# A graph network's first layer: node sums added one supertile later, edge products one group ahead, and a count check moved to ScalarE

## The chip, the core and the metric

The kernel runs on one core of one Trainium2 chip. The core has five engines with queues of their own, which work in order and wait for each other on semaphores: TensorE (PE; its weight loads are shown as PEld), VectorE (DVE), ScalarE (ACT), GpSimd (POOL) and SyncE (SP, here only a queue for transfers). The metric is the device time of one execution in microseconds; less is better. A profile is one further execution, recorded instruction by instruction.

## What is computed

Four graph layers over 6250 nodes with 64 features and 206250 edges sorted by destination (each node has itself as an edge too). Each layer's result is added to x and normalised. The change is in layer 0:

```python
def _L0_gnn_ref(H, Xe, id_Xe, M_W, M_b, U_W, U_b):
    features = H[id_Xe[0]]
    M_in = jnp.concatenate([features, Xe], axis=1)
    Y = jax.nn.relu(M_in @ M_W.T + M_b)
    Z = jax.ops.segment_sum(Y, id_Xe[1], num_segments=H.shape[0])
    U_in = jnp.concatenate([H, Z], axis=1)
    return jax.nn.relu(U_in @ U_W.T + U_b)

x = _layernorm(x + _L0_gnn_ref(x, edge_attr_64, edge_index, ...), axis=-1)
x = _layernorm(x + _L1_gnn_ref(x, edge_index, ...), axis=-1)   # two graph convolutions
x = _layernorm(x + _L2_gnn_ref(x, edge_attr_64, src, dst, ...), axis=-1)   # attention over edges
x = _layernorm(x + _L3_gnn_ref(x, edge_index, ...), axis=-1)   # two convolutions, batch norms
```

## The kernel before

**Tiling.** The edges are cut into S = 54 supertiles of L x J = 128 x 30 edges (the last has 91 partitions). Since edges are sorted by destination, a supertile's destinations fit a window of W = 128 nodes. Instructions keep the order in which the program writes them (a manual schedule), so each engine's queue is in program order; pools with 2 or 3 buffers decide how far one engine can run ahead of another.

**Layer 0's loop** (the loop over s at the end of the first printed part) does this for every supertile:

- `fetch_xe` loads 128 x 30 edge rows (one transfer, SP's queue, two buffers), and `fetch_g` gathers 128 x 30 rows of a node table by source: 30 indirect transfers, issued one by one by GpSimd (L433), into one of three buffers g.
- `messages` works on the supertile fetched one iteration earlier, in five groups of six edges a partition. For each group TensorE transposes the edge rows (L662), ScalarE copies the result out of PSUM (L666), TensorE multiplies by the edge weights into pm (L676), and VectorE adds pm's 64 columns to g (L680) and copies four attention columns to we (L682). The transposes run one group ahead of the products. After the five groups ScalarE applies relu to g (L687), and SP stores we to memory for layer 2 (L689).
- `add_window` sums by destination: VectorE makes two one-hot tiles oh, 15 edges a partition each (`one_hot`, L474), TensorE multiplies them with g in 60 instructions into one PSUM tile pa, of which there is one buffer (L484), and VectorE adds pa to the accumulator acc at the window's place (L487).
- In each group, `fill` also runs one step of another job, so that layer 0 and the preparation of later layers share the engines. For the first 11 iterations the job is `degrees`, five supertiles an iteration: two VectorE one-hots oA and oB a step (L524, L527; two buffers each) and 30 small matmuls of the step before (L518). After that it is `adjacency`: 200 steps that build dense count matrices of (source, destination) in one byte a count. A step makes the one-hots (L591, L594; the same oA and oB buffers), multiplies those of the step before (L603, 16 matmuls), has ScalarE cast the products to one-byte floats (L605, four casts), and checks the counts of the step before that.
- `check` (L610) takes on VectorE the largest of the 1568 bytes a partition, read as integers, into a column of most_a; at the end of the kernel this is compared with EXACT, the byte of the largest count that the format holds exactly, 15. Every eighth check is followed by a store of a finished adjacency chunk, on ScalarE's queue (L613). If any check of the kernel fails, a general but slow path at the end computes everything anew; otherwise its loop runs zero times.
- `last_messages` does the last supertile with one-hots made first, and with relu and sums after each group (L684, L700), and then adds pa (L705).

**What comes behind.** Layer 1 and layer 3 are dense products with the count matrices on TensorE (L862). Layer 2 gathers once more for each edge, with GpSimd issuing 30 transfers a supertile.

Of the kernel before, what the change touches and what calls it, by code (L numbers as in the profile page):

```python
# [27 lines left out]
F32 = mybir.dt.float32  # L28
BF16 = mybir.dt.bfloat16
FP8 = mybir.dt.float8e4  # L30
I32 = mybir.dt.int32
I8 = mybir.dt.int8
# [8 lines left out]
LF = 125  # L41
W = 128
R = 64
EXACT = 0x57 + 0.5
BIG = 1.0e30
LN_EPS = 1e-5
BN_EPS = 1e-5
# [8 lines left out]
def tile_gnn_resnorm(ctx: ExitStack, tc, a, out, J):  # L56
# [281 lines left out]
        return min(S, -(-(a_block * (b + 1) + SLACK + R) // LJ)) - 1  # L338

    nc.vector.memset(bad4, 0.0)  # L340

    w_bd = const.tile([128, 2, CW], F32, name="w_bd")
    nc.vector.memset(w_bd, 0.0)
# [82 lines left out]
    def of(s):  # L426

        return LP if isinstance(s, int) and s == S - 1 else L
# [46 lines left out]
                                rel[:, j0:j0 + JH, None].to_broadcast([n, JH, W]), op=OP.is_equal)  # L475
        return oh

    def add_window(ohp, vals, c, rel, base, places=iota):
        n = rel.shape[0]
        pa = sums_in[-1].tile([c, W], F32, name="pa")  # L480
        for j0 in range(0, J, JH):
            oh = one_hot(ohp, rel, j0, places)
            for j in range(JH):
                nc.tensor.matmul(pa, vals[0:n, j0 + j, 0:c], oh[0:n, j, :], start=(j0 + j == 0),  # L484
                                 stop=(j0 + j == J - 1))
        span = acc[0:c, ds(base, W)]
        nc.vector.tensor_add(span, span, pa)  # L487

    def first_of(s):
        why = "a destination, and the accumulator is a window longer than the nodes"  # L490
# [75 lines left out]
    def adjacency(adp, ohd):  # L566
# [40 lines left out]

        def check(c, q0, adj):

            nc.vector.tensor_reduce(most_a[:, (c * L + q0) // QS:(c * L + q0) // QS + 1],  # L610
                                    adj[:, :, :, q0:q0 + QS].bitcast(I8), AX.XYZ, OP.max)
            if q0 + QS == L:
                nc.scalar.dma_start(adj_d[c].bitcast(I8), adj.rearrange("p l a q -> p (l a q)").bitcast(I8))  # L613

# [25 lines left out]
    with st0:  # L640
# [7 lines left out]
            gather(g, D, tab_d, at(src_1 if s < S1 else src_sb, s))  # L648
            return g

        def fetch(s):
            return fetch_xe(s), fetch_g(s)

        def messages(pool, s, xe, g, first_time, fill=lambda: None, then=None):

            m = of(s)
            we = pool.tile([L, J, H], F32, name="we")

            def turned(k):
                pt = ps_t.tile([128, 3, L], F32, name="pt")  # L660
                for i in range(3):
                    nc.tensor.transpose(  # L662
                        pt[:, i, 0:m], xe[0:m, 6 * k + 2 * i:6 * k + 2 * i + 2, :].rearrange("p a c -> p (a c)"),
                        ident[:m, :m])
                xT = pool.tile([128, 3, L], F32, name="xT", bufs=3)
                nc.scalar.copy(xT[:, :, 0:m], pt[:, :, 0:m])  # L666
                return xT[:, :, 0:m]

            xTs = [turned(0)]
            for k in range(J // 6):  # L670
                if k + 1 < J // 6:
                    xTs.append(turned(k + 1))
                xT = xTs.pop(0)
                pm = ps_m.tile([L, 3, 2 * CW], F32, name="pm")
                for i in range(3):
                    nc.tensor.matmul(pm[0:m, i, :], xT[:, i, :], w_bd_f, start=True, stop=True)  # L676
                fill()
                pv = pm[0:m].rearrange("p i (a c) -> p (i a) c", a=2)
                js = slice(6 * k, 6 * k + 6)
                nc.vector.tensor_add(g[0:m, js, :], g[0:m, js, :], pv[:, :, 0:D])  # L680
                if first_time:
                    nc.vector.tensor_copy(we[0:m, js, :], pv[:, :, D:CW])  # L682
                if then:
                    nc.scalar.activation(g[0:m, js, :], g[0:m, js, :], AF.Relu)  # L684
                    then(js)
            if not then:
                nc.scalar.activation(g[0:m], g[0:m], AF.Relu)  # L687
            if first_time:
                nc.sync.dma_start(edges_of(we_d, s), we[0:m])  # L689
            return g  # L690

        def last_messages(s, xe, g):

            rel, n = at(dst_w, s), of(s)
            ohs = [one_hot(ohp, rel, j0, iota_c[:, 0:W]) for j0 in range(0, J, JH)]
            pa = sums_in[-1].tile([D, W], F32, name="pa")

            def add(js):
                for j in range(js.start, js.stop):
                    nc.tensor.matmul(pa, g[0:n, j, :], ohs[j // JH][0:n, j % JH, :], start=(j == 0), stop=(j == J - 1))  # L700

            base = first_of(s)
            messages(l0, s, xe, g, True, then=add)
            span = acc[0:D, ds(base, W)]
            nc.vector.tensor_add(span, span, pa)  # L705

        xes = [fetch_xe(i) for i in range(2)]
        got = xes[0], fetch_g(0)
        load_edges(src_i, src, S1)
        nc.sync.dma_start(hl_d[0:E, :].rearrange("(p i) k -> p i k", p=LF), hl)  # L710
        nc.sync.dma_start(rows_d[E:E + R, :], zero)
# [35 lines left out]

        x_part()

        add0 = lambda v, rel, base: add_window(ohp, v, D, rel, base, iota_c[:, 0:W])  # L750
        with ExitStack() as st1:
            adp = st1.enter_context(tc.tile_pool(name="adp", bufs=2))
            counting = degrees(ohd, list(range(S)))
            building = adjacency(adp, ohd)

            n_count = S // 5 + 1
            n_build = NC * L // QS + 2
            last, done = None, 0
            for s in range(S + 1):
                nxt = got if s == 0 else (xes[1], fetch_g(1)) if s == 1 else fetch(s) if s < S else None  # L760
                if s < n_count:
                    steps = [counting] * 5
                else:
                    upto = -(-n_build * (s - n_count + 1) // (S - n_count))
                    steps, done = [building] * (upto - done), upto

                def fill():
                    if steps:
                        next(steps.pop(), None)

                if s == S:
                    while steps:
                        fill()
                    for _ in building:
                        pass
                    last_messages(s - 1, *last)
                elif last:
                    v = messages(l0, s - 1, *last, True, fill)
                    add0(v, at(dst_w, s - 1), first_of(s - 1))
                while steps:  # L780
                    fill()
                last = nxt
    ps_0.close()
    ps_s = ctx.enter_context(tc.tile_pool(name="ps_s", bufs=2, space=PSUM))
    sums_in.append(ps_s)
# [467 lines left out]


    nc.vector.tensor_reduce(bad4[:, 2:3], most_a, AX.X, OP.max)
    for i, most_ok in enumerate((0.5, R + 0.5, EXACT, 0.5, 0.5)):
        nc.vector.tensor_scalar(bad4[:, i:i + 1], bad4[:, i:i + 1], most_ok, None, op0=OP.is_gt)
    bad1 = small.tile([L, 1], F32, name="bad1")
    nc.vector.tensor_reduce(bad1, bad4, AX.X, OP.max)
# [8 lines left out]
    with tc.For_i(0, n_bad, 1), tc.tile_pool(name="gen", bufs=2) as ag:  # L1268
# [9 lines left out]
        def message_sums(s):  # L1278
            xe = ag.tile([L, J, D], F32, name="xe", bufs=1)
            nc.sync.dma_start(xe[0:of(s)], edges_of(xe_in, s))  # L1280
            g = ag.tile([L, J, D], F32, name="g", bufs=1)
            gather(g, D, tab_d, row_of_edges(ag, src, s))
            windows(s, messages(ag, s, xe, g, False), lambda v, rel, base: add_window(ag, v, D, rel, base))

        all_supertiles(message_sums)

# [53 lines left out]
```

## Time and profile before

| | us |
|---|---|
| median of 3 runs (lowest, highest) | 7077.11 (7062.18, 7077.8) |
| the profiled execution | 5427.65 |
| its span | 5425.9 |
| layer 0's loop within the span | about 101 to 2351 |
| layer 2's gathers within the span | about 2702 to 4830 |

| engine | busy us in the span | share |
|---|---|---|
| GpSimd | 3168.7 | 58% |
| VectorE | 2808.8 | 52% |
| TensorE | 2154.0 | 40% |
| ScalarE | 782.1 | 14% |

In a line of a group or of the timeline stand: the kernel's line, the engine, the operation, what is written and read, partitions x elements, and how many. A group then gives its busy time, the mean of one in ns, and the engine's idle time just before with what ended it. A line of the waits is who waited, for whom, the sum in us, how often, and the longest. "issue" means that the profile shows nothing that the engine waited for; where a wait is long, that includes waits for a buffer that the queue itself carries. GpSimd's busy time is the issuing of a transfer, not the transfer.

### The profile page before, as it was taken

What the parts mean: (1) busy time and instruction counts of PE and PEld (TensorE: products, weight loads), DVE (VectorE), ACT (ScalarE), POOL (GpSimd) and SP (SyncE); (2) the same over time, 40 slices, a digit from 0 to 9 for tenths busy, and PEclk for the clock granted to TensorE, in tenths of its full rate; (3) what the DMA queues carried; (4) which work ended last, traced back from release to release, by engine and by line L of the source; (5) the groups of instructions that cost most, each with busy time, mean ns of one, the idle gap of its engine ahead of it and who ended that gap; (6) DMA issues with size and microseconds to landing.
All of it is one profiled execution on the core that took longest, in us unless ns stands there. A gap on an engine that the chain in (4) does not pass through costs nothing.

```text
span 5425.9 us, 42770 instructions
## 1 busy us (share of the span) xinstructions
PE 2154.0 (40%) x15765; PEld 1667.7 (31%) x15766; DVE 2808.8 (52%) x2743; ACT 782.1 (14%) x1615; POOL 3168.7 (58%) x3350
## 2 busy tenths in 40 slices
PE   2555555555555555589800000000000000019997
PEld 2545554454455445566500000000000000014554
DVE  5888788888878888841213334234243334421102
ACT  0001232232223223221100000000000000001101
POOL 6566767777767776500077777777777777740000
PEclk6766676677677677689955555555555555559998
DMA  4111222222222222247423233233333333335442
GB/s 101 43 47 47 69 72 73 80 72 73 74 78 73 73 68 71 70 173 275 169 68 123 85 112 112 85 123 101 108 101 110 98 102 123 101 101 214 155 167 72
DMA packets 200887, 551.26 MB, mean 102 GB/s; under 512 B 110150, under 2 KB 112466, under 8 KB 178396
## 3 DMA queue, kind: packets, MB, share of 16 engines
q0 software_dynamic: 112336, 219.94, 15.4%
q1 hardware_dynamic: 67908, 281.60, 13.9%
q10 hardware_dynamic: 20424, 46.89, 2.3%
q8 instruction: 126, 2.06, 0.1%
q14 instruction: 93, 0.76, 0.0%
HBM read 442.89 MB, written 105.30 MB: 101 GB/s over the span
## 4 chain that ended last, share of the span: by engine, by line
POOL 36%; PE 19%; issue 18%; DMA 14%; DVE 11%; ACT 2%; DVEq 0%; POOLq 0%; ACTq 0%; SPq 0%
POOL g L433 35%; PE pA L862 12%; DMA rows<-rows_d,first 9%; DMA g<-tab_d,src_sb 5%; PE pa L484 3%; DVE most_a L610 2%; DVE oB L594 2%; DVE oA L591 2%; ACT g L687 1%; DVE g L680 1%; DVE oA L524 1%; PE pm L845 1%; PE pm L189 1%; DVE oB L527 1%; POOL slots L439 0%
## 5 line engine op out<-in xcount | busy, mean ns | idle before, releaser
L433 POOL DMA_INDIRECT g<-tab_d,src_sb x3120 | 2947.9, 945 | 1553.4 <-issue 1044.1
L177 PE MATMUL pt<-ident,acc 128*128 128x128 f32 (+1 forms) x50 | 13.5, 364 | 1994.6 <-DVE acc L235 1994.6
L484 PE MATMUL pa<-oh,g 128*64 128x128 f32 x3180 | 472.6, 324 | 386.0 <-ACT g L687 377.1
L177 PEld LDWEIGHTS pt<-ident,acc 128*128 128x128 f32 (+1 forms) x50 | 7.1, 174 | 1999.8 <-issue 1986.4
L484 PEld LDWEIGHTS pa<-oh,g 128*64 128x64 f32 x3180 | 461.4, 170 | 395.9 <-ACT g L687 395.9
L862 PE MATMUL pA<-adj,three 128*128 128x512 fp8e4 (+3 forms) x2499 | 534.7, 368 | 1.8 <-ACT three L243 1.8
L1010 DVE TENSOR_TENSOR g<-g,we 128x120 f32<-128x120 f32 (+1 forms) x54 | 15.5, 286 | 887.6 <-DMA g<-tab_d,src_sb 887.6
L591 DVE TENSOR_TENSOR oA<-pc,hlT 128x2048 bf16<-128x2048 f32 x200 | 454.7, 2274 | 0.0
L605 ACT CAST adj<-pA 128x392 fp8e4<-128x392 f32 x800 | 350.2, 488 | 590.8 <-PE pA L603 585.8
L603 PE MATMUL pA<-oB,oA 128*128 128x98 bf16 x3200 | 292.1, 241 | 258.2 <-DVE oB L594 189.1
L594 DVE TENSOR_TENSOR oB<-pc,hlT 128x1568 bf16<-128x1568 f32 x200 | 354.5, 1773 | 0.0
L610 DVE TENSOR_REDUCE most_a<-adj 128x1 f32<-128x1568 int8 x200 | 353.7, 1769 | 0.0
L862 PEld LDWEIGHTS <-three 128*96 128x96 bf16 (+1 forms) x2548 | 267.9, 111 | 241.6 <-issue 13.1
L676 PE MATMUL pm<-w_bd,xT 128*128 128x136 f32 (+1 forms) x1620 | 324.7, 351 | 31.0 <-ACT xT L666 14.9
L1040 DVE TENSOR_REDUCE hb<-rows 128x64 f32<-128x4096 f32 x46 | 336.5, 7316 | 0.0
L603 PEld LDWEIGHTS <-oA 128*128 128x128 bf16 x3200 | 227.5, 117 | 322.2 <-DVE oB L594 207.5
L676 PEld LDWEIGHTS pm<-w_bd,xT 128*128 128x128 f32 (+1 forms) x1620 | 276.3, 245 | 61.4 <-DVE we L682 32.9
L1028 ACT COPY same<-pA 128x256 f32<-128x256 f32 x49 | 18.2, 372 | 1813.2 <-DVE pA L1026 1813.2
L1037 DVE TENSOR_TENSOR rows<-rows,pA 128x4096 f32<-128x4096 f32 x49 | 216.7, 4422 | 38.5 <-ACT pA L1035 38.5
L1026 DVE TENSOR_TENSOR pA<-rows,pa 128x256 f32<-128x256 f32 x49 | 21.0, 429 | 414.9 <-DMA rows<-rows_d,first 414.9
L474 DVE TENSOR_TENSOR oh<-pc,dst_w 128x1920 f32<-128x1920 f32 (+1 forms) x108 | 227.1, 2140 | 0.1
L666 ACT COPY xT<-pt 128x384 f32<-128x384 f32 (+1 forms) x270 | 124.0, 479 | 696.9 <-PE pt L662 696.2
(253 smaller groups left out, 2605.0 us busy)
## 6 DMA issues: line engine op xcount, KB each, us to landing
adj<-adj_d SPq DMA_DIRECT2D x100, 1568.0 KB
rows_d<-g SPq DMA_DIRECT2D x53, 1020.0 KB
xe<-in_edge_attr_dram SPq DMA_DIRECT2D x53, 960.0 KB
g<-tab_d,src_sb POOLq DMA_INDIRECT x3120
adj_d<-adj ACTq DMA_DIRECT2D x25, 1568.0 KB
we_d<-we SPq DMA_DIRECT2D x53, 60.0 KB
we<-we_d ACTq DMA_DIRECT2D x53, 60.0 KB
g<-tab_d,src POOLq DMA_INDIRECT x120
```

The lines of the kernel that those rows point to most:

```text
L433: nc.gpsimd.indirect_dma_start(out=g[0:n, j, 0:c], out_offset=None, in_=table[:, :], in_offset=bass.IndirectOffsetOnAxis(ap=idx[:, j:j + 1 ...
L474: nc.vector.tensor_tensor(oh[0:n], places[0:n, None, :].to_broadcast([n, JH, W]), rel[:, j0:j0 + JH, None].to_broadcast([n, JH, W]), op=OP ...
L484: nc.tensor.matmul(pa, vals[0:n, j0 + j, 0:c], oh[0:n, j, :], start=(j0 + j == 0), stop=(j0 + j == J - 1))
L591: nc.vector.tensor_tensor(o_h, iota_c[:, None, 1:L + 1].to_broadcast([128, QS, L]), hlT[:, 0, q0:q0 + QS, None].to_broadcast([128, QS, L]) ...
L594: nc.vector.tensor_tensor(o_l, iota_2[:, None, :].to_broadcast([128, QS, 2 * NB]), hlT[:, 1, q0:q0 + QS, None].to_broadcast([128, QS, 2 * ...
L603: nc.tensor.matmul(pA[:, q].rearrange("p a l -> p (a l)"), o_h[:, q1 + q, :], o_l[:, q1 + q, :], start=True, stop=True)
L605: nc.scalar.copy(adj[:, :, :, q0 + q1:q0 + q1 + 4], pA.rearrange("p q a l -> p l a q"), saturate=False)
L610: nc.vector.tensor_reduce(most_a[:, (c * L + q0) // QS:(c * L + q0) // QS + 1], adj[:, :, :, q0:q0 + QS].bitcast(I8), AX.XYZ, OP.max)
L676: nc.tensor.matmul(pm[0:m, i, :], xT[:, i, :], w_bd_f, start=True, stop=True)
L862: nc.tensor.matmul(pa[ps, 0:nk, 0:w], t[:, b, :], adj[:, 0:nk, b, 0:w], start=(b == 0 and t is part), stop=(b == NB - 1 and t is part))
L1037: nc.vector.tensor_mul(hn, hn, ex[:, :, :, None].to_broadcast([L, R, H, HD]))
L1040: nc.vector.tensor_reduce(hb[:, b, :], rows[:, :, 0:D].rearrange("p r c -> p c r"), AX.X, OP.add)
```

## The change

Five edits, all in layer 0's loop or for it:

1. `add_window` is split: `window_sums` does the matmuls into pa, `add_sums` the addition to acc. In the loop the addition of supertile s - 1 is carried over (`late_sum`) and made in group 1 of the next supertile's messages.
2. The two one-hot tiles for the sums are made in the last two groups (`fill` with k = 3 and 4) in place of after the messages.
3. `edge_products` is a running producer over all groups of all supertiles: `ahead` transposes two groups ahead and multiplies one group ahead, across the border between supertiles.
4. The counting job runs four steps an iteration, and so for 15 iterations (n_count).
5. The check is a ScalarE activation, relu of (count - 15), with a sum over the row into most_a; the limit at the end is 0.5.

```diff
-EXACT = 0x57 + 0.5
+MOST = 15.0
...
+    less = const.tile([L, 1], F32, name="less")
+    nc.vector.memset(less, -MOST)
...
+    def window_sums(pa, vals, oh, j0):
+        n, c = vals.shape[0], pa.shape[0]
+        for j in range(j0, j0 + JH):
+            nc.tensor.matmul(pa, vals[:, j, 0:c], oh[0:n, j - j0, :], start=(j == 0), stop=(j == J - 1))
+
+    def add_sums(pa, base):
+        span = acc[0:pa.shape[0], ds(base, W)]
+        nc.vector.tensor_add(span, span, pa)
...
         def check(c, q0, adj):
-            nc.vector.tensor_reduce(most_a[:, (c * L + q0) // QS:(c * L + q0) // QS + 1],
-                                    adj[:, :, :, q0:q0 + QS].bitcast(I8), AX.XYZ, OP.max)
+            above = adp.tile([L, NB, 2, QS], BF16, name="above", bufs=1)
+            nc.scalar.activation(above, adj[:, :, :, q0:q0 + QS], AF.Relu, bias=less[:, 0:1],
+                                 accum_out=most_a[:, (c * L + q0) // QS:(c * L + q0) // QS + 1])
...
+        def edge_products(pool, todo):
+            xTs, pms = [], []
+
+            def turn():
+                xe, m, k = next(todo, (None, 0, 0))
+                if xe is None:
+                    return
                 pt = ps_t.tile([128, 3, L], F32, name="pt")
...
                 nc.scalar.copy(xT[:, :, 0:m], pt[:, :, 0:m])
+                xTs.append(xT[:, :, 0:m])
+
+            def ahead():
+                turn()
+                if xTs:
+                    xT = xTs.pop(0)
+                    m = xT.shape[-1]
+                    pm = ps_m.tile([L, 3, 2 * CW], F32, name="pm")
+                    for i in range(3):
+                        nc.tensor.matmul(pm[0:m, i, :], xT[:, i, :], w_bd_f, start=True, stop=True)
+                    pms.append(pm[0:m])
+
+            turn()
+            ahead()
+            return ahead, pms
+
+        def messages(pool, s, g, products, first_time, fill=lambda k: None, then=None):
...
             for k in range(J // 6):
+                ahead()
+                fill(k)
+                pv = pms.pop(0).rearrange("p i (a c) -> p (i a) c", a=2)
...
-        def last_messages(s, xe, g):
+        def last_messages(s, g, products, before):
             ohs = [one_hot(ohp, rel, j0, iota_c[:, 0:W]) for j0 in range(0, J, JH)]
+            before()
...
-            n_count = S // 5 + 1
+            n_count = -(-S // 4) + 1
             n_build = NC * L // QS + 2
+            edge_p = edge_products(l0, ((xes[s], of(s), k) for s in range(S) for k in range(J // 6)))
+            g, done, late_sum = None, 0, None
             for s in range(S + 1):
+                if 1 < s < S:
+                    xes.append(fetch_xe(s))
+                g_next = g_0 if s == 0 else fetch_g(s) if s < S else None
                 if s < n_count:
-                    steps = [counting] * 5
+                    steps = [counting] * 4
...
+                def fill(k):
                     if steps:
                         next(steps.pop(), None)
+                    if k == 1:
+                        add_late()
+                    if k >= J // 6 - 2:
+                        ohs.append(one_hot(ohp, at(dst_w, s - 1), len(ohs) * JH, iota_c[:, 0:W]))
...
-                elif last:
-                    v = messages(l0, s - 1, *last, True, fill)
-                    add0(v, at(dst_w, s - 1), first_of(s - 1))
+                elif s:
+                    messages(l0, s - 1, g, edge_p, True, fill)
+                    pa = sums_in[-1].tile([D, W], F32, name="pa")
+                    for i, oh in enumerate(ohs):
+                        window_sums(pa, g, oh, i * JH)
+                    late_sum = pa, first_of(s - 1)
...
-    for i, most_ok in enumerate((0.5, R + 0.5, EXACT, 0.5, 0.5)):
+    for i, most_ok in enumerate((0.5, R + 0.5, 0.5, 0.5, 0.5)):
```

## The prediction, before the change was run

> **What bounds the kernel now.** I read the page first (sections 2 and 5), then the waits, the stretches and the timeline of layer 0's loop, about 101 to 2351 us of the 5425.9 us span.
>
> ```profile
> L433 POOL DMA_INDIRECT g<-tab_d,src_sb x3120 | 2947.9, 945 | 1553.4 <-issue 1044.1
> L591 DVE TENSOR_TENSOR oA<-pc,hlT 128x2048 bf16<-128x2048 f32 x200 | 454.7, 2274 | 0.0
> L605 ACT CAST adj<-pA 128x392 fp8e4<-128x392 f32 x800 | 350.2, 488 | 590.8 <-PE pA L603 585.8
> L594 DVE TENSOR_TENSOR oB<-pc,hlT 128x1568 bf16<-128x1568 f32 x200 | 354.5, 1773 | 0.0
> L610 DVE TENSOR_REDUCE most_a<-adj 128x1 f32<-128x1568 int8 x200 | 353.7, 1769 | 0.0
> ```
>
> These are the page's groups. The count check (L610) is 353.7 us of VectorE. The waits of 150 to 2280 us show what VectorE and GpSimd wait for:
>
> ```profile
> POOL g L433 <- issue: 615.1, 1475, 29.6
> DVE acc L487 <- PE pa L484: 357.2, 51, 7.8
> ACT g L687 <- DMA g<-tab_d,src_sb: 70.7, 12, 6.6
> ```
>
> VectorE stands idle 357 us, 7.0 us for each of 51 supertiles, until TensorE has the 60 node-sum matmuls that L487 adds. The busy shares of a late stretch, VectorE 81%, GpSimd 71%:
>
> ```profile
> core 0: us, PE busy (x) PEld busy (x) DVE busy (x) ACT busy (x) POOL busy (x), PEclk, DMA share, GB/s
> 1700.00:2200.00 500.00, 283.53 (x2221) 251.76 (x2220) 405.98 (x347) 146.23 (x298) 353.38 (x375) 0.71 0.24 73
> ```
>
> The timeline of the first supertile, and GpSimd's of a late one, show the chain:
>
> ```profile
> 160.35 4.21 DVE L474 TENSOR_TENSOR oh<-pc,dst_w 128x1920 f32<-128x1920 f32 x2
> 160.36 1.80 ACT L687 ACTIVATE g<-g 128x1920 f32<-128x1920 f32 x1 [16.40 <-DVE g L680]
> 162.59 8.79 PE L484 MATMUL pa<-oh,g 128*64 128x128 f32 x60 [7.47 <-ACT g L687]
> 171.48 0.28 DVE L487 TENSOR_TENSOR acc<-acc,pa 64x128 f32 x1 [6.93 <-PE pa L484]
> 172.12 0.94 POOL L433 DMA_INDIRECT g<-tab_d,src  x1 [29.58 <-issue]
> 173.36 0.94 POOL L433 DMA_INDIRECT g<-tab_d,src  x1 [0.30 <-issue]
> ...
> 2243.43 0.96 POOL L433 DMA_INDIRECT g<-tab_d,src_sb  x1 [6.04 <-issue]
> ```
>
> GpSimd issues a gather every 1.249 us (0.944 busy, 0.30 gap, whatever the others do) and stops once for each supertile, here 6.04 us, until the sums free one of three g buffers. So VectorE sets a supertile's time (41.3 us: L487's first start 171.5 and last 2318.5, over 52 intervals) and GpSimd is close behind it (30 gathers, 37.5 us; with 50 slot fetches over the build, 38.8).
>
> **A rule against the row.** The Trainium skill, Perfetto Trace Analysis, section Identifying the Most-Contended Engine, takes the occupancy of VectorE, ScalarE and GpSimd as a fair measure of their distance from the limit. By it GpSimd has 29% to spare, and VectorE's 354 us of check plus 357 us of waiting could nearly all come off: some 6400 us. By the row GpSimd is full at 0.944/1.249 = 76% busy, not at 100%. I take the row: room is 1670 issues (1620 gathers, 50 slots) from 22.8 us on: 2086 us, against the 2258 they take now. The gain at the last gather is at most 172 us.
>
> **The change, part by part**, per supertile, T being its last edge addition.
>
> *Node sums one supertile later.* The 60 matmuls stay where they are in TensorE's queue; only L487's addition (0.28 us) moves to group 1 of the next supertile. The 7.0 us wait does not all go. VectorE goes on with a step of group 0 (counting 4.1 + 1.6 = 5.7 us; building 2.2 + 1.7 = 3.9) and an edge addition with its copy (0.56), and then wants a one-hot buffer oA for group 1. There are two, and the older one's matmuls are in TensorE's queue behind the sums: sums end at T + 11.0 to 11.2 (171.4 against 160.4; 2198.7 against 2187.4), then transposes and products of the group ahead (0.5 + 0.9), then the step's own matmuls (0.9 counting, 1.65 building). VectorE restarts at T + 13.5 or 14.3, having come at 6.3 or 4.5. The new wait is 7 us while counting, 10 while building; behind it stand the late addition, all other edge additions and the one-hots, and then the relu, the sums and GpSimd's buffer. Only the work done meanwhile is saved.
>
> *One-hots among the last groups.* 2 x 2.1 us, before T instead of after; no saving of VectorE's time, and the relu starts 4.2 us later in the supertile than it would.
>
> *Edge products one group ahead.* No instruction more. VectorE waits for pm now in only 3 places (3.2 us), so nothing in the loop; in the last supertile it takes transposes and products out of each group's chain. The edge rows' DMA still stands behind the we_d store on SP's queue (it issues at 160.91 now), and a group is wanted 1 group sooner, some 25 us after that: hidden.
>
> *Four counting steps in place of five.* 5.7 us less in each of 14 supertiles; 202 building steps now go over 39 supertiles (5.2 each) instead of 43.
>
> *The check on ScalarE.* VectorE loses 5.2 x 1.77 = 9.2 us per building supertile. ScalarE gains 200 activations over 1568 elements with a sum. No such row exists. The cast of 392 (0.488 us) and the relu of 1920 (1.802) give 0.86 ns an element, 1.5 us; a second small instruction for the sum would add about 0.25 (the 128x49 activation at L213). The other end: the Trainium skill, ScalarE: Activation LUTs, Rules for kernel authors, says of relu and max to use VectorE, which is up to about 3 times faster, so 3 x 1.77 = 5.3 us. The VectorE row is 1.1 ns an element, so no faster mode is at work in it; I take 1.6 us. ScalarE then has 5.2 x (4 x 0.488 + 1.6) + 5 x 0.48 + 1.8 = 22.7 us per supertile: hidden in 38.8. The adj_d stores stay on its queue behind the check, 25 in 2 ms: hidden. At 5.3 us it would be 41.9 and nothing is hidden.
>
> *A supertile after.* Counting: 13.5 + 6.5 + 6.3 + 8.4 + 2.7 = 37.4 us (groups 1 to 4, with the one-hots), against GpSimd's 37.5. Building: 14.3 + 4.8 + 4.5 + 6.6 + 6.6 + 0.8 (a sixth step now and then) = 37.6, against GpSimd's 38.8. GpSimd now sets the time, by about 1 us; what is late next is the gather.
>
> *The sum.* The first supertile starts two times 5.7 us sooner, but carries the 4.2 us of one-hots before its relu: its buffer is free near 165 us, not 172.1. GpSimd has 1580 issues left: 165 + 1973 = 2138, and I allow 12 us where a supertile overruns it: last gather at 2150, now 2280.8. Then now come 70 us to L705's end at 2350.8, since VectorE is one supertile behind and the last five groups take 6.0 us each. After: landing about 2, five groups of TensorE's 5.1 us or less (23 in all), ends: 28 us, 2178. Gain 172 us, 3.2% of the profiled execution.
>
> **Profile and median.** That execution took 5427.65 us (the span and 1.75 around it); the median of the runs is 7077.11, 1649 us more, and no view shows where. I carry the 172 us over one for one: 6905 us.
>
> **The rivals.**
> *A, the gathers already bound the timed runs.* If the 1649 us lie in the 3339 indirect DMAs of the two gathering stages, one costs (7077 - 1040)/3339 = 1.81 us (1040 = span less the 2258 and 2128 us of those stages), a supertile 54 us, and VectorE's 41 are hidden already. Only the tail is left: 7070. For it: GpSimd's stages are 4.4 of 5.4 ms, and no other single cause reaches 1649 easily. Against: the trace shows 0.94 us with no spread, under any load. Partly so, anything between.
> *B, the removed wait comes back whole.* If oA's wait, queue jitter and the later relu make a supertile 40 us, the loop ends near 23 + 54 x 40 + 80 = 2263 less a little: gain about 70 to 90, 6995.
> *C, slower: the check on ScalarE.* Place: between the casts and the relu in ScalarE's queue. It decides from 5.2 us a check on: 14.3 + 5.2 X exceeds 41.3 there. At 5.3, 0.6 x 39 = 23 us slower, 7100; at 6, 7240. For it: the skill's rule, and 16-byte runs of one-byte input. Against: the 0.86 ns row.
> *D.* The change not doing what it says: the sums do move and the check goes, by the code; the flag test only changes its limit. Small.
>
> **How the numbers follow.** Main case 0.48, 6905, its own range 6870 to 6960. B 0.12. A 0.25, 7070, which is no change. C and anything else slower 0.15. About 0.3% (21 us) is what a measurement of this kernel can tell from none. Range 6870 to 7085: main, B and A, leaving out C and a little. Faster 0.60, same 0.25, slower 0.15.
>
> **What would show it.** Right: L610 gone from VectorE; the addition's wait for pa near 0, a new wait of VectorE at L524/L591 for L518/L603 of 7 to 10 us; GpSimd's gaps all 0.30 after the first stop; VectorE waiting for g; last gather near 2150 and loop end near 2178; ScalarE's check 1.5 to 1.9 us. Wrong: GpSimd still stopping 3 us or more for each supertile (B), checks over 5 us (C), or a profile 170 us shorter with timed runs the same (A).

## The result and the profile after

| | median us | lowest to highest | runs |
|---|---|---|---|
| before | 7072.80 | 7061.35 to 7082.36 | 12 |
| after | 7080.98 | 7073.18 to 7087.70 | 12 |

The ratio after to before is 1.0012, with a 95% interval of 1.0004 to 1.0021: no change that this measurement can tell from none, where 6905 us and a gain were forecast. The measured 7081 us lies just inside the forecast's range of 6870 to 7085, at the end that stood there for rival A.

The profiled execution of after has a span of 7085.8 us. It is not a faster copy of the profile of before (5425.9 us): it is 1660 us longer, although no engine does that much more (VectorE 2482 us busy in place of 2809, GpSimd 3315 in place of 3169). The experiments below show what differs: the profile of before agrees with the times of one chip (e17, e18), the timed runs with those of three others (e1 to e16). First the page's groups of after:

```profile
L435 POOL DMA_INDIRECT g<-tab_d,src_sb x3120 | 3084.8, 989 | 3016.5 <-issue 2553.4
L599 DVE TENSOR_TENSOR oA<-pc,hlT 128x2048 bf16<-128x2048 f32 x200 | 457.7, 2288 | 1486.1 <-PE pA L611 1086.9
L611 PE MATMUL pA<-oB,oA 128*128 128x98 bf16 x3200 | 314.4, 249 | 1377.4 <-issue 891.3
L613 ACT CAST adj<-pA 128x392 fp8e4<-128x392 f32 x800 | 360.6, 488 | 1448.2 <-remote 999.3
L619 ACT ACTIVATE above<-adj,less 128x1568 bf16<-128x1568 fp8e4 x200 | 320.9, 1604 | 0.0
```

The busy times are as forecast: the check is an activation of 1604 ns (L619), the one-hot oA takes 2288 ns (2274 before). What is new is idle time, and it is everywhere at once: VectorE 1486 us before L599 where there was none, ScalarE 1448 us before its casts in place of 591, TensorE 1377 us before L611, which waits mostly for "issue", for nothing that the profile shows. Then the waits of layer 0's loop of after (150 to 3700 us; sum, times, longest):

```profile
POOL g L435 <- issue: 2045.7, 1467, 74.9
DVE oA L599 <- PE pA L611: 1037.5, 80, 30.0
PE pA L611 <- issue: 865.9, 116, 27.5
DVE oA L532 <- remote: 469.3, 23, 31.7
```

("remote" stands for a releaser that this core's profile does not show.) VectorE's wait for pa (357 us before) is gone, and waits for oA have taken its place, as forecast, but with up to 30 us apiece and not 7 to 10. GpSimd, forecast to be the engine that sets the pace, stops for some 33 us in each supertile. TensorE's timeline in one supertile's gathers shows the source (start, length, matmuls, idle before):

```profile
1033.06 0.20 PE L526 MATMUL pA<-oB,oA 91*128 91x49 bf16 x1 [1.90 <-issue]
1035.86 0.20 PE L526 MATMUL pA<-oB,oA 91*128 91x49 bf16 x1 [2.60 <-issue]
1038.66 0.20 PE L526 MATMUL pA<-oB,oA 91*128 91x49 bf16 x1 [2.60 <-issue]
...
1046.36 0.20 PE L526 MATMUL pA<-oB,oA 91*128 91x49 bf16 x1 [1.20 <-issue]
1047.06 0.20 PE L526 MATMUL pA<-oB,oA 91*128 91x49 bf16 x1 [0.50 <-issue]
1047.76 0.74 PE L526 MATMUL pA<-oB,oA 91*128 91x49 bf16 x14 [0.50 <-issue]
```

These matmuls belong to one step, and in the last row 14 of them start 0.04 us apart, with nothing to wait for. While GpSimd gathers they start singly, 0.7, 1.4, 2.1 or 2.8 us apart. GpSimd's timeline and the stretches of the same supertile:

```profile
1041.62 0.94 POOL L435 DMA_INDIRECT g<-tab_d,src_sb  x1 [0.30 <-issue]
1071.36 0.94 POOL L435 DMA_INDIRECT g<-tab_d,src_sb  x1 [28.80 <-issue]
```

```profile
core 0: us, PE busy (x) PEld busy (x) DVE busy (x) ACT busy (x) POOL busy (x), PEclk, DMA share, GB/s
1005.00:1042.00 37.00, 10.03 (x98) 6.88 (x96) 6.61 (x7) 0.96 (x2) 27.73 (x30) 0.58 0.11 25
1048.00:1071.00 23.00, 14.85 (x99) 13.56 (x96) 11.24 (x40) 4.55 (x6) 0.00 (x0) 0.69 0.13 46
```

In 37 us with 30 gathers VectorE does 7 instructions and ScalarE 2; in the 23 us behind them, with no gather, 40 and 6. The DMA engines are 11% busy meanwhile, so their bandwidth isn't the limit. The granted clock, 0.58 against 0.69, is too near for starts of up to 2.8 us apart in place of 0.04. The hold-up begins and ends some 4 us behind the gathers: counted from 4 us after a supertile's first gather to 4 us after its last, TensorE starts 0.90 matmuls a us over layer 0's loop, and 4.83 a us in the rest; in the profile of before it was 4.2 and 8.2. Counted while gathers are being issued, without that shift, it is 1.9 and 3.8. All rates among the gathers below are counted with the shift. So in this execution gathers and TensorE's work largely take turns: 37.5 us of gathers plus some 33 us of the rest, 71.7 us a supertile while counting and 70.0 while building; this is called the stall below. In the profile of before they lay beside each other, 41 us.

### The profile page after: what moved, and what is told of

Same layout as the page of the kernel before. It is cut to its first block, busy times and chain, and to the rows that moved or that the text cites. A ratio compares the mean times of both kernels' runs of the same rounds, so it can differ in the third digit from the quotient of the medians.

```text
span 7085.8 us, 42975 instructions
## 1 busy us (share of the span) xinstructions
PE 2260.4 (32%) x15765; PEld 1738.2 (25%) x15766; DVE 2482.3 (35%) x2544; ACT 1102.4 (16%) x2015; POOL 3315.0 (47%) x3350
## 4 chain that ended last, share of the span: by engine, by line
POOL 20%; PE 19%; issue 15%; another core or an unknown queue 15%; DVE 7%; ACT 5%; DMA 3%; DVEq 0%; POOLq 0%; ACTq 0%
POOL g L435 20%; PE pA L902 9%; PE pa L484 5%; DVE oB L602 2%; DMA rows<-rows_d,first 2%; DVE oA L599 2%; ACT adj L613 2%; ACT above L619 1%; PE pA L611 1%; ACT g L710 1%; DVE oh L476 1%; DMA g<-tab_d,src_sb 1%; PE pt L672 1%; PE pm L686 1%
## 5 line engine op out<-in xcount | busy, mean ns | idle before, releaser
L435 POOL DMA_INDIRECT g<-tab_d,src_sb x3120 | 3084.8, 989 | 3016.5 <-issue 2553.4
L599 DVE TENSOR_TENSOR oA<-pc,hlT 128x2048 bf16<-128x2048 f32 x200 | 457.7, 2288 | 1486.1 <-PE pA L611 1086.9
L611 PE MATMUL pA<-oB,oA 128*128 128x98 bf16 x3200 | 314.4, 249 | 1377.4 <-issue 891.3
L611 PEld LDWEIGHTS <-oA 128*128 128x128 bf16 x3200 | 250.8, 122 | 1439.6 <-issue 1428.7
L686 PE MATMUL pm<-w_bd,xT 128*128 128x136 f32 (+1 forms) x1620 | 353.5, 370 | 255.6 <-DVE we L705 233.8
L532 DVE TENSOR_TENSOR oA<-pc,dst_h 128x3840 bf16<-128x3840 f32 x54 | 224.3, 4155 | 469.3 <-remote 469.3
L686 PEld LDWEIGHTS pm<-w_bd,xT 128*128 128x128 f32 (+1 forms) x1620 | 301.6, 264 | 288.8 <-issue 173.2
L619 ACT ACTIVATE above<-adj,less 128x1568 bf16<-128x1568 fp8e4 x200 | 320.9, 1604 | 0.0
```

The costliest lines, as they stand in the source:

```text
L435: nc.gpsimd.indirect_dma_start(out=g[0:n, j, 0:c], out_offset=None, in_=table[:, :], in_offset=bass.IndirectOffsetOnAxis(ap=idx[:, j:j + 1 ...
L532: nc.vector.tensor_tensor(o_h, iota_c[:L, None, 0:L].to_broadcast([L, J, L]), dst_h[:, s, :, None].to_broadcast([L, J, L]), op=OP.is_equal)
L599: nc.vector.tensor_tensor(o_h, iota_c[:, None, 1:L + 1].to_broadcast([128, QS, L]), hlT[:, 0, q0:q0 + QS, None].to_broadcast([128, QS, L]) ...
L611: nc.tensor.matmul(pA[:, q].rearrange("p a l -> p (a l)"), o_h[:, q1 + q, :], o_l[:, q1 + q, :], start=True, stop=True)
L619: nc.scalar.activation(above, adj[:, :, :, q0:q0 + QS], AF.Relu, bias=less[:, 0:1], accum_out=most_a[:, (c * L + q0) // QS:(c * L + q0) // ...
```

## The experiments

Runs of one group (e1 to e4, e5 to e8, e9 to e12, e13 to e16, e17 and e18) ran on one chip beside the kernel before; e9 to e16 share a chip. Each chip but that one was met on one occasion only, so "chip" below can't be told from "occasion". e13, e14, e16, e17 and e18 ran four times (0.1 to 0.7% from lowest to highest), the others once. "A supertile" is the mean spacing of GpSimd's first gather (or transfer), while counting and while building.

| run | us | before, same chip | supertile, us |
|---|---|---|---|
| e1 before again | 7086.4 | 7086.1 | 73.0 / 68.6 |
| e2 after, one plain transfer | 5348.6 | 7086.1 | 36.2 / 37.3 |
| e3, e4 after, 30 plain transfers | 5346.1, 5345.3 | 7086.1 | |
| e5 before, one plain transfer | 5615.8 | 7018.1 | 42.5 / 41.2 |
| e6 after, 15 gathers | 5834.8 | 7018.1 | |
| e7 after, rows in order | 7032.7 | 7018.1 | |
| e8 after, 3 oA/oB, 2 g | 6825.3 | 7018.1 | 64.8 / 65.4 |
| e9 after, memset 128x512 | 6053.2 | 7079.9 | 49.8 / 51.3 |
| e10 after, memset 128x1 | 7102.5 | 7079.9 | |
| e11 after, bursts of ten | 6289.4 | 7079.9 | |
| e12 e8 with early one-hots | 6820.1 | 7079.9 | 61.4 / 66.3 |
| e13 after, memset 128x256 | 5938.4 | 7082.8 | 48.0 / 48.2 |
| e14 before, memset 128x256 | 6048.6 | 7082.8 | 53.5 / 48.6 |
| e15 after, memset 128x128 | 6824.4 | 7082.8 | 65.0 / 65.4 |
| e16 after, check on VectorE | 7217.8 | 7082.8 | 71.6 / 73.1 |
| e17 after, five counting steps | 5275.1 | 5428.0 | 41.7 / 38.8 |
| e18 e13 with 3 oA/oB, 2 g | 5594.4 | 5428.0 | 43.3 / 44.8 |

**Is it the gathers? (e1 to e4)**

*e1*, the kernel before, unchanged:

> The kernel before once more, for a trace at the time of its timed runs. Theory 1 (TensorE hardly starts an instruction while GpSimd issues layer 0's gathers, as in the profile after: 0.9 matmuls a us then, 4.8 outside): about 7070 us, and the trace shows the same two rates and some 70 us from one supertile's gathers to the next. Theory 2 (the kernel before has no such stop; its 1649 us lie elsewhere): about 7070 us with a supertile near 42 us and the time in another stage, or 5430 us as in the profile shown.

It took 7086.4 us, and its trace shows the turns too: 0.91 matmul starts a us among the gathers, 4.85 in the rest. So the change didn't bring them. Its waits (150 to 3700 us):

```profile
POOL g L433 <- issue: 2046.9, 1480, 80.5
DVE acc L487 <- PE pa L484: 357.3, 51, 7.8
```

GpSimd stops for 2047 us, not for the 615 that the prediction was made from (the 0.30 us gaps are in both); the pa wait of 357 us is there in both.

*e2, e3, e4*, the gathers replaced by plain transfers:

```diff
-            gather(g, D, tab_d, at(src_1 if s < S1 else src_sb, s))
+            nc.gpsimd.dma_start(g[0:of(s)], edges_of(xe_in, s))                       # e2
+            for j in range(J):                                                        # e3; e4: nc.sync
+                nc.gpsimd.dma_start(g[0:of(s), j, :], edges_of(xe_in, s)[:, j, :])
```

> Layer 0's 30 gathers of a supertile are replaced by one plain transfer of the same bytes, issued by GpSimd (edge rows in place of node rows, so the sums are of other numbers). Theory 1: no stop of TensorE is left; a supertile takes what VectorE and TensorE need, 34 to 38 us as the prediction worked out, layer 0 ends near 2050 and the whole takes 5250 to 5500 us. Theory 2 (the stop comes from TensorE's own instructions or from the other transfers): 6800 us or more, TensorE still below 1 matmul a us in stretches.

> The 30 gathers are replaced by 30 plain transfers of 128 rows of 256 bytes each, also issued by GpSimd (edge rows in place of node rows). If issuing by GpSimd is what stops TensorE: about 7000 us, 0.9 matmuls a us while they are issued. If the indirection or the scattered rows are: 5250 to 5500 us.

> The same 30 plain transfers issued by SyncE in place of GpSimd. If the number of small transfers and of their completions is what stops TensorE: about 7000 us. If it is GpSimd's way of issuing: 5250 to 5500 us.

All three take 5345 to 5349 us, 1740 less than before on the same chip. So neither 30 instructions, nor GpSimd issuing them, nor 256-byte pieces hold TensorE up; the gathers do. In e3 the plain transfers even follow each other faster than the gathers, every 0.53 us. The group of e3's plain transfers, and a wait of e2 (150 to 2000 us):

```profile
L658 POOL DMA_DIRECT2D g<-in_edge_attr_dram x1620 | 860.4, 560 | 1085.8 <-issue 920.3 <-PE pt L673 111.4 <-DMA g<-in_edge_attr_dram 50.5
```

```profile
DVE oA L599 <- PE pA L611: 288.5, 46, 9.9
```

The second is the oA wait that the prediction named: 9.9 us at most, where it put 10 for every building supertile, and 6.3 on average.

**What the change is worth with no gathers (e5), half of them (e6), other rows (e7)**

*e5* is e2's edit on the kernel before.

> The kernel before, with layer 0's 30 gathers a supertile replaced by one plain transfer of the edge rows on GpSimd's queue (so layer 0 adds up other rows than the reference's). It is the counterpart of e2 (the same edit on the changed kernel: 5348.6 us, layer-2 gathers from 2438.7 us of the span). What the change is worth where TensorE isn't held up: the profile of before that was shown had no hold-up and was bound by VectorE at 41.3 us a supertile, its layer-2 gathers began at 2701 us. Theory 1 (the change works as forecast on VectorE, and is only covered by the hold-up): layer-2 gathers from 2640 to 2710 us, 5550 to 5620 us in all, so 200 to 270 us slower than e2. Rival (the oA wait gives all of it back, with or without the hold-up): within 25 us of e2, 5325 to 5375.

It takes 5615.8 us: the change is worth 267 us there (e2 ran on another chip, but layer 2's gathers take 2304 and 2306 us in the two, and begin 268 us later in e5, so the difference lies ahead of them), 42.5 to 36.2 us a supertile while counting and 41.2 to 37.3 while building. The forecast was 37.4 and 37.6 for VectorE's side of it. So the rival by which the oA wait gives all back is out.

*e6*, gathers for the even columns only, one plain transfer for the others:

```diff
+            nc.gpsimd.dma_start(g[0:n, 1:J:2, :], edges_of(xe_in, s)[:, 1:J:2, :])
+            for j in range(0, J, 2):
+                nc.gpsimd.indirect_dma_start(
```

> The kernel after, with 15 of the 30 gathers of each supertile in layer 0 (the even columns) and one plain transfer of edge rows for the odd columns (other rows than the reference's there). Theory 1 (TensorE is held up for as long as GpSimd issues gathers, 1.25 us each, and the rest of a supertile comes behind that): 54 x 15 x 1.25 = 1012 us less than 7086, about 6070. Rival (the hold-up comes only when many gathers are outstanding at once): 5345 to 5500, as with none. Rival (any gather slows the whole supertile): above 6700.

5834.8 us: the first 15 gathers cost some 490 us over e2, the next 15 some 1200 (to e7's 7033 on this chip; e2 ran on another). That is less than the forecast 6070, and not linear: the first gathers of a supertile cost TensorE little. The traces agree. Taken by the time since a supertile's first gather, TensorE in the kernel after starts 2.5 to 3.9 matmuls a us from 2.5 to 10 us, 1.6 at 10, and only 0.2 to 0.4 from 17 to 40 us, and recovers within 5 us of the last gather. A backlog that builds up would look like this; it became theory 2.

*e7*, the same gathers with the table's rows in order:

```diff
-            gather(g, D, tab_d, at(src_1 if s < S1 else src_sb, s))
+            gather(g, D, tab_d, seq_i[0:of(s)])
```

> The kernel after, with the 30 gathers of each supertile reading the table's rows in order (gather j reads rows 128 j to 128 j + 127, the same for each supertile, so other rows than the reference's). Instructions, sizes and queues are as in the kernel after; only the addresses are no longer scattered. Theory 1a (the indirect instruction itself holds TensorE up): 7040 to 7120. Theory 1b (the scattered rows of the table do): near the plain transfers' 5346, at most 5600.

7032.7 us (before: 7018.1), 1.08 matmul starts a us among the gathers. It goes with the indirect instruction, not with the scattered addresses.

**Taking turns, used (e8, e12)**

```diff
-    ohd = st0.enter_context(tc.tile_pool(name="ohd", bufs=2))
+    ohd = st0.enter_context(tc.tile_pool(name="ohd", bufs=3))
-    gp = st0.enter_context(tc.tile_pool(name="gp", bufs=3))
+    gp = st0.enter_context(tc.tile_pool(name="gp", bufs=2))
```

> The kernel after, with three buffers of the one-hots oA and oB in place of two (and two gather buffers g in place of three, to make room). Theory 1 (gathers and TensorE's work take turns, so what counts is how fast TensorE's turn goes; VectorE can now make one step more during the gathers, and the 9.4 to 9.7 us wait for oA behind the sums goes): a supertile 4 to 6 us shorter, 6750 to 6870 us. Rival (TensorE's own rate sets its turn): 7060 to 7100. Rival (the third g buffer was needed): over 7150.

6825.3 us, 2.7% less than before on its chip. While building, VectorE starts 2.0 steps among a supertile's gathers in place of after's 1.1 (counted in the traces by writes of oA), and a supertile loses 5 to 7 us. Forecast 6750 to 6870.

*e12* also makes the sums' one-hots in groups 0 and 1 (`if k < 2:` in `fill`):

> The kernel of e8 (three buffers of oA and oB, two of g) with the two one-hot tiles for the sums made in groups 0 and 1 in place of 3 and 4. Theory 1 (gathers and TensorE take turns, VectorE's work that falls among the gathers is free): 4.3 us of VectorE's work moves from TensorE's turn to the gathers', 2 to 4.3 us less a supertile, 6590 to 6720 us. Rival (TensorE's turn is set by TensorE): within 40 us of e8's 6825.

6820.1 us, on another chip than e8, so the two can't be compared to a fraction of a per cent. By their traces counting lost 3.4 us a supertile (64.8 to 61.4) and building gained 0.9. VectorE's waits (150 to 3500 us) show what came instead:

```profile
DVE oh L476 <- PE pa L484: 306.1, 46, 34.8
```

The early one-hot wants its buffer back from sums that TensorE has not finished. The forecast of 6590 to 6720 was missed, and the time is the one of the rival (within 40 us of e8). VectorE's work moved into the gathers helps only if its buffers are free.

**The pace of the gathers (e9, e10, e11, e15)**

```diff
+    spare = pk.tile([128, 512], F32, name="spare")
...
             for j in range(J):
                 nc.gpsimd.indirect_dma_start(...)
+                nc.gpsimd.memset(spare, 0.0)
```

> The kernel after, with one GpSimd memset of a spare 128x512 tile behind each gather of layer 0. By the one memset row of its trace (64x6400 in 5.42 us, 0.85 ns an element) it takes about 0.45 us, with its gap 0.5 to 0.6; a gather then comes every 1.8 us in place of 1.25, 30 in 54 us. Theory 2 (TensorE is held up by a backlog that builds up because gathers are issued a little faster than something drains them: in the kernel after, TensorE starts 2.5 to 3.9 instructions a us in the first 10 us of the gathers and 0.2 to 0.4 from 17 us on): the backlog doesn't form, TensorE runs beside the gathers, a supertile is about 55 to 58 us: 6290 to 6450 us in all. Rival (TensorE is held up as long as gathers are being issued, at any pace): 54 + 33 = 87 us a supertile, 8000 us.

6053.2 us, 14.5% less than before on the same chip (one run each), from slower gathers; better than the 6290 to 6450 expected. GpSimd's timeline of e9:

```profile
1500.27 0.95 POOL L660 DMA_INDIRECT g<-tab_d,src_sb  x1 [0.17 <-issue]
1501.22 0.55 POOL L663 MEMSET spare<- 128x512 f32 x1
1501.93 0.95 POOL L660 DMA_INDIRECT g<-tab_d,src_sb  x1 [0.16 <-issue]
```

A gather comes every 1.66 us. TensorE starts 4.0 matmuls a us among the gathers, nearly the 4.2 of the profile of before, and 50 to 51 us a supertile is GpSimd's own pace (30 x 1.66 = 49.8, and 50 slot fetches over the building stage). VectorE now waits for g, whose data come last (150 to 2800 us):

```profile
DVE g L709 <- DMA g<-tab_d,src_sb: 800.6, 184, 9.5
DVE oA L600 <- PE pA L612: 129.0, 35, 9.8
```

> The same with the smallest memset (one element a partition, 0.11 us by the trace's rows, with its gap some 0.2): a gather every 1.4 to 1.45 us, 30 in 43 us. Theory 2: less backlog than at 1.25, between 45 us a supertile (5750 us in all, if 1.43 is slow enough) and 70 (7086, if it isn't). Rival (as long as gathers are issued): 43 + 33 = 76 us a supertile, 7400 us.

7102.5 us, but this was no test of 1.43 us: the memset of one element takes 0.118 us, fits into the 0.30 us gap behind a gather, and the median spacing stayed at 1.252 us.

> The kernel after, with the gathers in three bursts of ten at the old pace, each burst followed by ten memsets of the spare 128x512 tile (5 to 6 us in all): 30 gathers in 53 to 55 us. Theory 2 (backlog that drains in the pauses; TensorE recovers 2.5 to 5 us after the last gather in the kernel after): 55 to 60 us a supertile, 6290 to 6560. Rival (as long as gathers are issued): TensorE runs only in the pauses of 6 us, 12 of them inside, so 54 + 33 - 12 = 75 us a supertile, 7360.

6289.4 us: three bursts of ten at the old pace with pauses between do nearly as well as even spacing. With turns at any pace it would have been 7360. So it behaves like a backlog that drains in the pauses of some 6 us; no view shows what piles up.

> The kernel after with memsets of 128x128: about 0.22 us, a gather every 1.33 us, 30 in 40 us. If TensorE is free already at 1.33: a supertile of about 41 us, 5480 to 5570 us in all. If the backlog still forms: 6300 to 7100.

6824.4 us at about 1.33 us a gather, 65 us a supertile: TensorE is still held up. Of the rivals, that was the one expected at 6300 to 7100.

**The change with spaced gathers (e13, e14)**

The edit is e9's with 256 columns in place of 512 (in e15 128, in e10 one).

> The kernel after with a memset of a spare 128x256 tile behind each gather of layer 0: by e9's rows (0.95 us a gather, 0.546 for 128x512, 0.118 for one element, 0.16 gap) about 0.33 us, so a gather every 1.44 us, 30 in 43.3 us, 44.7 with a slot fetch. If that is slow enough for TensorE (theory 2): GpSimd sets the supertile, 44 to 45 us, layer 0's last gather near 2400 to 2450 us of the span, 5670 to 5740 in all. If it isn't: TensorE stalls as in the kernel after, a supertile of 43 + 33 = 76 us, 7400; in between, anything.

5938.4 us; the ratio to before is 0.8389, 95% interval 0.8371 to 0.8407. Better than either kernel, and better than e9, but above the forecast 5670 to 5740: at 1.44 us a gather a supertile takes 48 us, not 44 to 45. Part of the hold-up is left (150 to 2700 us):

```profile
DVE oA L600 <- PE pA L612: 421.3, 50, 17.9
PE pA L612 <- issue: 364.7, 214, 9.0
```

> The kernel before with the same memsets. If GpSimd sets the pace of both at 44 to 45 us a supertile (VectorE's 41.3 of the profile that was shown is less than that): within 1.5% of e13, the rest being the end of the loop (about 50 us). Rival (VectorE's waits add to GpSimd's pace, the change is worth what it was without gathers, 267 us): 5930 to 6000 us.

6048.6 us, ratio to before 0.8548 (0.8526 to 0.8571). That is above both forecasts. With spaced gathers the change is worth 110 us, 1.8%: some 80 of them by the end of the counting stage (53.5 to 48.0 us a supertile), little while building (48.6 to 48.2), and the rest at the loop's end. By e18, below, GpSimd's own pace is 44.8 us there.

**The check, under the stall (e16)**

```diff
-            nc.scalar.activation(above, adj[:, :, :, q0:q0 + QS], AF.Relu, bias=less[:, 0:1], accum_out=...)
+            nc.vector.tensor_reduce(..., adj[:, :, :, q0:q0 + QS].bitcast(I8), AX.XYZ, OP.max)
```

> The kernel after with the count check back on VectorE (the maximum of the bytes, as before), the other four edits kept. Theory 1 (gathers and TensorE take turns, and VectorE's work lies mostly beside the gathers): within 0.5% of the kernel before and after, 7040 to 7110. Rival (ScalarE's check costs TensorE's turn about what VectorE's saved, so each part counts): faster than before by 1% or more. Rival (the check on ScalarE does pay, and another edit eats it): slower than before by 1% or more.

7217.8 us, 1.019 of before (1.0176 to 1.0205): the four other edits together cost 1.9%, or 135 us, on a chip that stalls. With the check on ScalarE too the ratio is 1.0012, so moving the check is worth 1.8%, some 126 us (73.1 to 70.0 us in each of 39 building supertiles is 121; the kernel after ran elsewhere, so the ratios to before are compared). My first explanation, that VectorE's work is simply free while TensorE stalls, falls: the measured zero is a gain and a loss that cancel.

**Five counting steps, and a chip without the stall (e17, e18)**

```diff
-            n_count = -(-S // 4) + 1
+            n_count = S // 5 + 1
-                    steps = [counting] * 4
+                    steps = [counting] * 5
```

> The kernel after with five counting steps a supertile, as before (11 supertiles of counting, then 43 of building with 4.7 steps in place of 39 with 5.2); the other four edits kept. If the four steps eat the gain of the check: a counting supertile about 73 us, a building one 67 to 68.5 in place of 70, so layer 0 is 60 to 100 us shorter, 6980 to 7020 us in all (against 7081 for the kernels before and after). If the late sums, the early one-hots or the products ahead eat it: 7060 to 7100.

> The kernel of e13 (a 128x256 memset behind each gather, 5938 us) with three buffers of oA and oB and two of g. If VectorE's 8 us wait for oA is what keeps a supertile at 47 to 50 us: it falls to GpSimd's pace of 44.7 to 46 us, 5760 to 5860 us in all. Rival (with two g buffers the gathers of a supertile wait for the sums of the one before last, and the slack between GpSimd and the rest is gone): 6000 to 6500 us.

The chip of these two doesn't stall: seven runs of the kernel before took 5424.8 to 5432.0 us there, around the 5427.65 of the profile that was shown. So neither answers the question it was run for. e17 answers the larger one. It takes 5275.1 us, 0.9714 of before (0.9698 to 0.9731): 153 us faster with four edits of the five. VectorE's waits (150 to 2280 us), GpSimd's in the building stage (1000 to 1500 us), and the busy times of a late stretch:

```profile
DVE oA L599 <- PE pA L611: 259.2, 53, 10.1
DVE g L703 <- DMA g<-tab_d,src_sb: 160.8, 57, 6.9
DVE oA L532 <- PE pA L526: 57.5, 9, 7.3
```

```profile
POOL g L435 <- issue: 112.8, 370, 0.3
```

```profile
core 0: us, PE busy (x) PEld busy (x) DVE busy (x) ACT busy (x) POOL busy (x), PEclk, DMA share, GB/s
1700.00:2200.00 500.00, 294.57 (x2256) 260.00 (x2256) 313.86 (x306) 230.99 (x411) 365.42 (x387) 0.72 0.26 81
```

In e17's building stage GpSimd never waits longer than the 0.3 us between two gathers: it issues one every 1.249 us, with two slot fetches in every other supertile or so, 38.8 us a supertile. While counting it still stops for 4 to 5 us in each supertile. e18 is 3.0% slower than before there (1.0303, 1.0286 to 1.032): a supertile takes 43.3 us while counting and 44.8 while building, and 30 gathers every 1.44 us are 43.2, so where nothing stalls, spacing only slows the engine that sets the pace.

## Why the prediction was wrong, point by point

**The step that failed** is "I carry the 172 us over one for one". The sum was made on a profile of 5427.65 us and added to runs of 7077. The 1649 us between them were named and left unexplained. They were no constant beside the loop: they are the loop itself, on a chip where TensorE starts 0.91 matmuls a us among the gathers in place of 4.2 (e1: layer 0's last gather at 3733.7 us in place of 2279.8, so 1454 of the 1649 us; most of the rest is in layer 2, whose supertiles are spaced 42.7 us there and 39.5 in the profile). A gain worked out for one bound was subtracted from a time with another. In its place the runs showed two effects that cancel: the check is worth some 126 us, the four other edits cost 135 (e16).

**Right on the chip that the profile describes.** e17 shows it, with five counting steps instead of four:

- *Building supertile 38.8 us, GpSimd setting it.* Measured 38.8, with no wait of GpSimd over 0.3 us.
- *The oA wait behind the sums.* It is there, 259 us in 53 waits, at most 10.1 us; the forecast 10 us was its upper end, the mean is 4.9.
- *VectorE waiting for g, gaps of 0.30 us on GpSimd.* Both while building; with five counting steps GpSimd still stops while counting.
- *Gain 172 us.* 153 with a counting stage of 41.7 us a supertile; the four steps of counting, forecast at 37.4 and measured at 36.2 in e2 with no gathers, were not run on this chip. Layer 2's first gather, at 2701 us before, is at 2544.5.

**The check on ScalarE.** Forecast 1.6 us, measured 1.604 (and a read of the sum, 0.19). The Trainium skill (ScalarE: Activation LUTs, Rules for kernel authors) sends relu and max to VectorE, up to about three times faster per element, but it says so of bf16 and of VectorE's 4x mode. The prediction left that condition out when it took 5.3 us as its other end. VectorE's row over the same one-byte counts was 1.769 us, so the page's figure had no bearing here. The 1.6 us from the rows was right, rival C is out, and e16 shows the move worth some 126 us even under the stall.

**The occupancy rule** (the Trainium skill, Perfetto Trace Analysis, Identifying the Most-Contended Engine). The row stood against it rightly: at 73% busy (365.42 of 500 us, e17's stretch of 1700 to 2200) GpSimd issues without a stop, and is full.

**Rival A** had the right result, no change, by luck, and the wrong mechanism. It put the missing time into the gathers themselves, 1.81 us each, with VectorE hidden behind them. Layer 0's gathers still come every 1.249 us; GpSimd stands idle for nearly half of each supertile. What is slow is TensorE, and VectorE is not hidden. The test "a profile 170 us shorter with timed runs the same" was not met either: the profile of after was 1660 us longer.

**Rival B** fell: e5 against e2, and e17.

**Why zero, then?** Under the stall the check gains some 126 us (e16), and the other edits lose about as much. Which of them isn't settled: the run for it met a chip without the stall. The traces point to two. One is the four counting steps: one step less shortens a stalled counting supertile by 1.3 us only (73.0 to 71.7), and moves 0.5 of a step into each building supertile. In e1 a building supertile with four steps takes 65.2 us and one with five 70.4 (12 and 25 of them), so a step costs 5.2 us there; by an estimate from these figures the new split costs some 95 of the 135 us. The other is the late sums: VectorE now makes one step while TensorE sums, and among the gathers it then starts 1.1 steps in e16 and 1.9 in e1. That is argued, not shown; the early one-hots remain possible too.

**Left open:** what the gathers and TensorE share, and why three chips here show it and one doesn't. No view shows the resource; the DMA engines are 11% busy in the stretch shown above. Transfers of instructions are no likely rival: those of 16 KB take 1.05 us on average in e1 and 1.06 in e17, where nothing stalls.

## What to carry to other kernels

When a profile and the timed runs differ by more than the effect sought, the first thing to find out is where the difference lies; a sum made on the one is no forecast for the other. Look at what each engine does in the stretches where another engine issues indirect transfers: if TensorE's matmuls start singly with "issue" before them, try spacing the gathers. Here a dummy memset of 0.33 us behind each one made the kernel 16% faster than before (e13), and 3% slower than before, in e18's variant with other buffers, on a chip that doesn't stall; so measure on several chips before keeping it.

## What the runs showed of the hardware

- Indirect gathers of 128 rows of 256 bytes, issued every 1.249 us, bring TensorE down to 0.8 to 1.1 matmul starts a us on three chips (e1, e7, e10, e16; 4.5 to 5.1 in the rest of the supertile), with starts mostly a multiple of 0.70 us apart; on a fourth chip (e17) it starts 4.9. Plain transfers of the same size and number don't do it (e3), and the order of the rows makes little difference (e7).
- The first ten or so gathers after a pause cost little (e11), and the effect is gone about 5 us after the last (the kernel after). At 1.33 us a gather it is still there (65 us a supertile), at 1.44 mostly gone (48), at 1.66 gone (50 to 51, GpSimd's own pace); all of that on one chip.
- A GpSimd memset of one element behind a gather (0.118 us) doesn't change the pace, 1.252 us: it fits into the 0.30 us gap (e10).
- Layer 2's gathers too differ by chip: a supertile of them takes 39.5 us in e17, 42.7 in e13, and GpSimd is busy with one for 0.95 us on average in e17, 1.03 in e13.
